# A two-layer decoder on one Trainium2 core: in the second causal attention the softmax division moves from the output to the exponentials, on GpSimd, and the norms' weights are applied while queries and keys are copied

## The chip, the cores and the metric

The kernel runs on one core of one Trainium2 chip. A core has five engines with queues of their own, each worked off in order: TensorE for matrix products (PE in the profile, its weight loads PEld), VectorE (DVE), ScalarE (ACT), GpSimd (POOL) and SyncE (SP), which here starts transfers. PE writes its results to PSUM, which DVE and ACT read; the other tiles lie in SBUF. The metric is device microseconds of one execution, the median of several.

## The reference

Two layers, each of self attention, a second sub-layer against a context, and a feed-forward part; after each of the six, the sum with its input is normalised over the 512 features. The change concerns the second layer's causal self attention alone (32 heads of 16 features, 8 sequences of 128 tokens; `x` is `(8, 128, 512)`):

```python
def _layer_norm(x, w, b):
    mu = jnp.mean(x, axis=-1, keepdims=True)
    var = jnp.mean(jnp.square(x - mu), axis=-1, keepdims=True)
    return (x - mu) * jax.lax.rsqrt(var + LN_EPS) * w + b
qkv = jnp.clip(jnp.einsum('bsd,ed->bse', hidden_states, Wqkv), -CLIP_QKV, CLIP_QKV)
q, k, v = jnp.split(qkv, [D_MODEL, 2 * D_MODEL], axis=-1)
q = _layer_norm(q, q_ln_w, q_ln_b)
k = _layer_norm(k, k_ln_w, k_ln_b)
...
scores = jnp.einsum('bqhd,bkhd->bhqk', q, k) * HEAD_DIM ** (-0.5)
scores = scores + slopes[None, :, None, None] * rel[None, None]
scores = jnp.where(causal[None, None], scores, jnp.float32(-1e+30))
probs = jax.nn.softmax(scores, axis=-1)
out = jnp.einsum('bhqk,bkhd->bqhd', probs, v).reshape(B, S, D_MODEL)
return jnp.einsum('bsd,ed->bse', out, Wout)
```

## The kernel before

All arithmetic is in fp32. The program is written as a sequence of instructions for named engines. The framework's planner then fixes each engine's order: of the instructions that its own cost estimates hold to be ready, the one written first goes first; `issue_after` puts an instruction behind another on its engine. It also puts in the waits between engines.

**The loop of the second attention** (the last loop that the printed functions show, over `b` and `f in (0, 2)`) makes two passes for each of the 8 batch items. A pass treats 16 heads, as two blocks of 128 features ("units"), with the class `Heads16`, which the first layer's attention uses too:

- Its constructor makes the scores: 32 small matrix products (L164) of a block of `qT` (queries turned, features by tokens) and of `kbd`. `kbd` holds the turned keys twice, each time with one of every two heads set to zero, so that one product serves two heads. DVE adds the bias (L672) into the tile `e` and takes the maxima (L181), each in two halves of the four row groups `r`. A row of `e` has 384 columns: two heads by 128 keys for the later 64 queries ("part" 0), two heads by 64 keys for the earlier ones (part 1).
- `exps(half)`: eight exponentials on ACT (L193), in place, each with its sum into `su`.
- `turn()`, one pass later: the reciprocal of the sums (DVE, L202), copied out to 16 columns a head by POOL (`rb`, L205); 12 transposes of `e` on PE (L212), copied to `pT` by DVE and ACT (L213); two transposes of `rb` on PE (L218), copied to `rT` by ACT (L220).
- `out()`, two passes later: probabilities times values (L229, L235), and the product with `rT` on DVE (L240) into `oT`. So the division of the softmax is done on the output, transposed.

Between these, each pass prepares the next item. In pass f=0: `normed` for queries and for keys. PE makes the projection (L86), DVE clips it (L627), takes the moments (L91 to L95), POOL the power (`rs`, L97), DVE subtracts the mean and scales (L631), and POOL multiplies by the norm's weights (L632) and adds its offsets (L633). `lnv` holds the four vectors of 512, the same in all partitions; it is loaded once (L609), and its two parts for queries are scaled by POOL (L611). The keys' last steps are put among the next pass's maxima (`keys_late`). In pass f=2: `values` (L646), the turned tokens of the item after, and `turned_both`: four transposes of the queries, copied to `qT` by DVE (L137); four of the keys, which DVE copies to `kbd` in one product with `pair`, the two masks of heads (L657). `projection` multiplies the previous item's `oT` by the output weights in two halves (L665), around `turned_both`, then adds and normalises (L103, L91 to L107).

`ps1` has four PSUM banks used in turn by most products; `ps2` two pairs of banks, used in turn by the scores and by the transposes of `e`.

Of the kernel before, what the change touches and what calls it, by code (L numbers as in the profile page):

```python
# [11 lines left out]
F32 = mybir.dt.float32  # L12
AF = mybir.ActivationFunctionType
ALU = mybir.AluOpType
# [3 lines left out]
P = 128  # L18
B, S, D = 8, 128, 512
NC = D // P  # L20
H, HD = 32, 16
# [17 lines left out]
def bc(ap, shape):  # L39
    return ap.to_broadcast(shape)  # L40
# [3 lines left out]
def decoder(ctx: ExitStack, tc: tile.TileContext, a: dict, out: bass.AP):  # L44
    nc = tc.nc
# [4 lines left out]
    sm = ctx.enter_context(tc.tile_pool(name="sm", bufs=4))  # L50
# [6 lines left out]
    def bank(name):  # L57
        return ps1.tile([P, 512], F32, tag="ps1", name=name)
# [14 lines left out]
    ident = glob.tile([P, P], F32, tag="ident", name="ident")  # L73
# [6 lines left out]
    pair = masks[:, C_HEAD : C_HEAD + 2]  # L80
# [65 lines left out]
    class Heads16:  # L146
# [5 lines left out]

        W = 3 * P

        def __init__(self, pool, units, bias, o_dst, name, between=()):
            self.pool, self.units, self.o_dst, self.name = pool, units, o_dst, name
            s = [banks(f"s_{name}_{i}") for i in range(2)]
            for part, cols, keys in ((0, slice(0, 2 * P), P), (1, slice(2 * P, 3 * P), 64)):  # L160
                for r in range(4):
                    rows = slice(32 * r, 32 * r + 32)
                    for u, (qT, kbd, _, _) in enumerate(units):
                        nc.tensor.matmul(  # L164
                            s[r // 2][64 * u : 64 * u + 64, r % 2, cols],
                            lhsT=qT[rows, 64 - 64 * part : P - 64 * part], rhs=kbd[rows, :, :keys],
                            start=True, stop=True,
                        )
# [19 lines left out]
        def exps(self, half):  # L188
            for part in range(2):
                e = self.by_heads(part)  # L190
                for r in (2 * half, 2 * half + 1):
                    for x in range(2):
# [2 lines left out]
                            bias=self.m[:, part, r, x : x + 1], accum_out=self.su[:, part, r, x : x + 1],  # L195
                        )

        def turn(self):


            rc = sm.tile([P, 16], F32, tag="rc", name=f"rc_{self.name}")
            nc.vector.reciprocal(rc, self.su.rearrange("p a r x -> p (a r x)"))  # L202

            rb = self.pool.tile([P, 2, 8, HD], F32, tag="rb", name=f"rb_{self.name}", bufs=1)
            nc.gpsimd.tensor_copy(rb, bc(rc.rearrange("p (a h) -> p a h", a=2).unsqueeze(3), [P, 2, 8, HD]))  # L205
            self.pT = self.pool.tile([P, 4, self.W], F32, tag="pT", name=f"pT_{self.name}", bufs=1)
            for i in range(2):
                pt = banks(f"pt_{self.name}_{i}")
                for r in range(2):
                    for k in range(3):  # L210
                        cols = slice(k * P, (k + 1) * P)
                        nc.tensor.transpose(pt[:, r, cols], self.e[:, 2 * i + r, cols], ident)  # L212
                (nc.scalar.copy if i else nc.vector.tensor_copy)(  # L213
                    self.pT[:, 2 * i : 2 * i + 2, :], pt[:, :, : self.W]
                )
            pr = bank(f"pr_{self.name}")
            for a in range(2):
                nc.tensor.transpose(pr[:, a * P : (a + 1) * P], rb[:, a].rearrange("p h d -> p (h d)"), ident)  # L218
            self.rT = self.pool.tile([P, 2, P], F32, tag="rT", name=f"rT_{self.name}", bufs=1)
            nc.scalar.copy(self.rT, pr[:, : 2 * P].rearrange("p (a q) -> p a q", a=2))  # L220

        def out(self):
            o = bank(f"o_{self.name}")
            for u, (_, _, v, vd) in enumerate(self.units):
                v, vd = (t() if callable(t) else t for t in (v, vd))
                late = slice(u * P + 64, u * P + P)
                for x in range(2):
                    for r in range(4):
                        nc.tensor.matmul(  # L229
                            o[32 * r : 32 * r + 32, late],  # L230
                            lhsT=v[:, 48 * r + 16 * x : 48 * r + 16 * x + 32],
                            rhs=self.pT[:, r, x * P + 64 * u : x * P + 64 * u + 64], start=(x == 0), stop=(x == 1),
                        )
                for r in range(4):
                    nc.tensor.matmul(  # L235
                        o[32 * r : 32 * r + 32, u * P : u * P + 64],
                        lhsT=vd[:, 32 * r : 32 * r + 32],
                        rhs=self.pT[:, r, 2 * P + 64 * u : 2 * P + 64 * u + 64], start=True, stop=True,
                    )
            nc.vector.tensor_tensor(  # L240
                self.o_dst.rearrange("p u (a q) -> p u a q", a=2),
                o[:, : 2 * P].rearrange("p (u a q) -> p u a q", u=2, a=2),
                self.rT[:, ::-1].rearrange("p a (u q) -> p u a q", u=2),
                ALU.mult,
            )
# [251 lines left out]
    for n, (p, f) in enumerate(steps):  # L497
        if f == 0:
            oTs.append(ap.tile([P, 2, NC, P], F32, tag="oT", name=f"oT0_{p}"))
        qT, kbd = qk  # L500
        units = []
# [4 lines left out]
        now = Heads16(ap, units, causal_bias, oTs[p][:, :, f, :], f"a0_{p}_{f}")  # L506
# [40 lines left out]
    kp = layer.enter_context(stage("a1k", 1))  # L547
# [57 lines left out]

    alibi = kp.tile([P, 2, 4, 3 * P], F32, tag="alibi", name="alibi")
    nc.sync.dma_start(alibi, a["alibi"])
    lnv = kp.tile([P, 4, D], F32, tag="lnv", name="lnv")
    nc.sync.dma_start(lnv, a["L1_ln"].partition_broadcast(P))  # L609

    nc.gpsimd.tensor_scalar(lnv[:, 0:2, :], lnv[:, 0:2, :], SCALE, None, ALU.mult)  # L611

    v_bufs = [values_tiles(qp, i) for i in range(2)]

# [5 lines left out]
    def normed(i, b, xT, later=None):  # L620


        n, w = (("q", w1q), ("k", w1k))[i]
        pq = bank(f"p{n}1_{b}")
        mm_acc(pq, [(xT[:, c, :], w[:, c, :]) for c in range(NC)])
        q = qp.tile([P, D], F32, tag=n, name=f"{n}1_{b}")
        nc.vector.tensor_scalar(q, pq, 8.0, -8.0, ALU.min, ALU.max)  # L627
        mean, rs = moments(q, f"{n}1_{b}")

        def normalized():  # L630
            done = nc.vector.tensor_scalar(q, q, mean, rs, ALU.subtract, ALU.mult)  # L631
# [17 lines left out]

    def turned_both(b, q, k):  # L650
        qT = ap.tile([P, NC, P], F32, tag="qT", name=f"qT1_{b}")
        transposed(q, NC, P, qT, f"qT1_{b}", "v")
        pt = bank(f"pTk1_{b}")
        for c in range(NC):
            nc.tensor.transpose(pt[:, c * P : (c + 1) * P], k[:, c * P : (c + 1) * P], ident)
        kbd = ap.tile([P, 2, D], F32, tag="kbd", name=f"kbd1_{b}")
        nc.vector.tensor_tensor(kbd, bc(pt.unsqueeze(1), [P, 2, D]), bc(pair.unsqueeze(2), [P, 2, D]), ALU.mult)  # L657
        return qT, kbd

    def projection(b, oT):  # L660
# [64 lines left out]
    v = values(0, xT)  # L725
# [75 lines left out]
    for b in range(B):  # L801
        qT, kbd = qk
        v_now = v
        oT = ap.tile([P, NC, P], F32, tag="oT", name=f"oT1_{b}")
        for f in (0, 2):
            units = []
# [19 lines left out]
                front.go(1)  # L826
            if prev:
                prev.turn()
            now.exps(1)
            half = projection(b - 1, oT_before) if f == 2 and b else iter((0, 0))  # L830
            next(half)
            if b + 1 < B:
                if f == 0:
                    raw.append(normed(1, b + 1, xT, keys_late))
                else:
                    qk = turned_both(b + 1, *raw)
            if b == B - 1:
                front.go(1)
            next(half)
# [314 lines left out]
def _layouts(i):  # L1154
# [16 lines left out]
        "vecs": np.stack(  # L1171
            [cols(i[k]) for k in ("L0_attn_bq", "L0_attn_bk")], axis=1
        ),
        "L1_ln": np.stack([i[f"L1_attn_{k}"] for k in ("q_ln_w", "q_ln_b", "k_ln_w", "k_ln_b")]),
        "L0_bvo": np.stack([i["L0_attn_bv"], i["L0_attn_bo"]]),
        "F0_base": _rows(i["L0_ffn_base_W"]),
        "F0_lora": np.concatenate(
# [7 lines left out]
            axis=1,  # L1185
# [38 lines left out]
```

## Time and profile before

| | us |
|---|---|
| median of the runs shown (902.07, 903.83, 905.71) | 903.83 |
| the profiled execution | 900.43 |
| its span, first to last instruction | 898.5 |
| PE busy in it | 863.2 (96%) |
| DVE busy | 564.9 (63%) |
| ACT busy | 361.7 (40%) |
| POOL busy | 166.1 (18%) |

The busy shares are means over stages with different limits; for a change in one stage the stage's own rows count. The second attention takes about 323 to 510 us. A row of the timeline gives start, duration, engine, line, operation, names of the tiles written and read, partitions by elements, and in brackets how long the engine had been idle before and whom it waited for. DVE instructions overlap a little: the next one can start some 0.1 us before the end of the row above. The groups by line give busy time and, after the comma, the mean duration in ns.

### The profile page before, as it was taken

The page shows a single profiled execution, that of the slowest core. Times are in us where ns is not written, and L with a number is a line of the kernel's source. Part 1 is how long each engine was busy: PE and PEld are TensorE (multiplying, and loading weights), DVE is VectorE, ACT ScalarE, POOL GpSimd, SP SyncE. Part 2 cuts the span into 40 slices and gives each one's busy share as a digit, 9 for nine tenths or more (in the row PEclk, how much of TensorE's full clock was granted, in tenths as well). Part 3 has the DMA queues.
Part 4 walks back from the last instruction along what each step waited for, and adds up shares of the span by engine and source line. Part 5 has one row for each costly group of instructions (what it writes and reads, how often), then busy time and mean ns, then how long its engine had stood idle before and what let it go on. Part 6 is the DMA issues. An engine that isn't in the chain of part 4 may idle for free.

```text
span 898.5 us, 16975 instructions
## 1 busy us (share of the span) xinstructions
PE 863.2 (96%) x6494; PEld 535.1 (60%) x6494; DVE 564.9 (63%) x1310; ACT 361.7 (40%) x1517; POOL 166.1 (18%) x235
## 2 busy tenths in 40 slices
PE   9999999999899999999999999999999999989985
PEld 5766655654455455555556687756576566764542
DVE  3757787776969567888888405635454444456744
ACT  3787464654222115766666313213122212233210
POOL 2401233132533413333333000000000000000001
PEclk9999999999999999999999999999999999989898
DMA  9700000130300002000012210422232212124220
GB/s 330 314 2 25 2 18 9 47 106 1 153 1 24 1 1 95 2 1 1 2 43 101 63 34 15 103 47 48 47 72 48 54 42 57 43 46 102 72 71 35
DMA packets 29779, 51.19 MB, mean 57 GB/s; under 512 B 5250, under 2 KB 21762, under 8 KB 27778
## 3 DMA queue, kind: packets, MB, share of 16 engines
q1 hardware_dynamic: 27138, 48.00, 17.9%
q10 hardware_dynamic: 2560, 2.10, 1.1%
q8 instruction: 51, 0.84, 0.4%
q14 instruction: 30, 0.25, 0.1%
HBM read 31.21 MB, written 2.10 MB: 37 GB/s over the span
## 4 chain that ended last, share of the span: by engine, by line
PE 68%; DVE 16%; ACT 9%; SPq 3%; issue 1%; POOL 1%; DMA 1%; POOLq 0%; DVEq 0%; ACTq 0%
PE pox L86 9%; ACT e_a L193 5%; PE pq L86 5%; PE pkx L86 5%; PE pqx L86 5%; PE pk L86 4%; PE pv L86 4%; PE o_x L924 4%; PE pof L86 4%; PE pvx L86 3%; SPq L914 3%; PE pt_a L212 3%; PE s_x L879 3%; PE po L665 2%; PE s_a L164 2%; DVE e_x L907 2%
## 5 line engine op out<-in xcount | busy, mean ns | idle before, releaser
L193 ACT ACTIVATE e_a<-e_a,m_a 128x128 f32<-128x128 f32 (+1 forms) x512 | 184.8, 365 | 113.7 <-DVE m_a L181 113.7
L900 ACT ACTIVATE e_x<-s_x,m_x 128x256 f32<-128x256 f32 x128 | 58.6, 483 | 141.6 <-DVE m_x L890 107.5
L193 ACT ACTIVATION_READ_ACCUMULATOR e_a<-e_a,m_a 128x1 f32 x512 | 97.6, 191 | 0.0
L86 PE MATMUL pox<-w_X_o,oTx 128*128 128x512 f32 x192 | 84.5, 597 | 0.0
L86 PE MATMUL pqx<-xTx,w_X_q 128*128 128x256 f32 x384 | 84.3, 380 | 0.0
L86 PEld LDWEIGHTS pqx<-xTx,w_X_q 128*128 128x128 f32 x384 | 72.7, 190 | 10.8 <-issue 1.0
L889 DVE TENSOR_REDUCE m_x<-s_x 128x4 f32<-128x1024 f32 x32 | 37.6, 1215 | 49.6 <-PE s_x L879 49.6
L86 PEld LDWEIGHTS pox<-w_X_o,oTx 128*128 128x128 f32 x192 | 35.8, 190 | 48.8 <-issue 48.8
L181 DVE TENSOR_REDUCE m_a<-e_a 128x4 f32<-128x512 f32 (+1 forms) x128 | 62.6, 542 | 0.0
L97 POOL TENSOR_TENSOR rs_x<-ve_x,neghalf 128x1 f32<-128x1 f32 x8 | 4.4, 548 | 307.6 <-DVE ve_x L95 307.6
L879 PE MATMUL s_x<-kTx,qTx 32*128 32x256 f32 x768 | 52.3, 391 | 3.3 <-ACT e_x L900 3.3
L212 PE MATMUL pt_a<-ident,e_a 128*128 128x128 f32 x384 | 48.6, 274 | 4.9 <-DVE e_a L352 3.9
L879 PEld LDWEIGHTS s_x<-kTx,qTx 32*128 32x128 f32 x768 | 41.4, 188 | 16.6 <-issue 9.2
L212 PEld LDWEIGHTS pt_a<-ident,e_a 128*128 128x128 f32 x384 | 43.5, 141 | 12.8 <-DVE e_a L352 4.9
L103 DVE TENSOR_TENSOR x_x<-pox,x_a 128x512 f32<-128x512 f32 x8 | 5.5, 691 | 65.7 <-PE pox L86 65.7
L924 PE MATMUL o_x<-pT_x,vx 128*32 128x512 f32 x384 | 43.3, 595 | 1.4 <-DVE oTx L930 1.4
L908 DVE STREAM_TRANSPOSE e_x<-e_x 128x1024 f32<-128x1024 f32 x32 | 39.7, 1240 | 0.8
L792 ACT COPY qTx<-pqx 128x512 f32<-128x512 f32 x24 | 14.1, 589 | 63.2 <-PE pqx L86 63.2
L907 DVE TENSOR_SCALAR e_x<-e_x,rc_x 128x256 f32<-128x256 f32 x128 | 36.3, 347 | 3.4 <-DVE rc_x L904 1.8
L164 PEld LDWEIGHTS s_a<-kbd,qT 32*64 32x64 f32 x1024 | 20.8, 131 | 28.0 <-issue 8.9
L164 PE MATMUL s_a<-kbd,qT 32*64 32x256 f32 (+1 forms) x1024 | 33.3, 335 | 1.7 <-DVE pT_a L213 0.8
L202 DVE RECIPROCAL rc_a<-su_a 128x16 f32<-128x16 f32 x32 | 8.0, 251 | 40.5 <-ACT e_a L193 40.5
(206 smaller groups left out, 1647.3 us busy)
## 6 DMA issues: line engine op xcount, KB each, us to landing
pT_x<-e_x SPq DMA_DIRECT2D x224, 64.0 KB, 2.0
w_X_q<-in_X_q SPq DMA_DIRECT2D x3, 1024.0 KB, 5.2
w_X_o<-in_X_o SPq DMA_DIRECT2D x3, 1024.0 KB, 5.0
w_L_Wv<-in_L_Wv SPq DMA_DIRECT2D x2, 1024.0 KB, 6.2
w_L_Wo<-in_L_Wo SPq DMA_DIRECT2D x2, 1024.0 KB, 7.8
x_in<-in_x SPq DMA_DIRECT2D x8, 256.0 KB, 8.5
ct<-in_ctx SPq DMA_DIRECT2D x8, 256.0 KB, 4.4
cT<-in_ctxT SPq DMA_DIRECT2D x4, 512.0 KB, 3.9
```

Source lines behind the costliest of these rows:

```text
L86: nc.tensor.matmul(ps, lhsT=l, rhs=r, start=(i == 0), stop=(i == n - 1))
L164: nc.tensor.matmul(s[r // 2][64 * u : 64 * u + 64, r % 2, cols], lhsT=qT[rows, 64 - 64 * part : P - 64 * part], rhs=kbd[rows, :, :keys], s ...
L181: self.scored = nc.vector.tensor_reduce(self.m[:, part, rs, :], self.by_heads(part)[:, rs], AX.X, ALU.max, negate=True)
L193: nc.scalar.activation(e[:, r, x, :], e[:, r, x, :], AF.Exp, bias=self.m[:, part, r, x : x + 1], accum_out=self.su[:, part, r, x : x + 1],)
L212: nc.tensor.transpose(pt[:, r, cols], self.e[:, 2 * i + r, cols], ident)
L879: nc.tensor.matmul(sc[g // 2][:, g % 2, u * 256 : (u + 1) * 256], lhsT=qT[rows, (h0 + u) * NS + n, :], rhs=kT[rows, n], start=(n == 0), st ...
L889: nc.vector.tensor_reduce(m, self.s[i], AX.X, ALU.max, negate=True)
L900: nc.scalar.activation(self.e[:, :, j, :], self.s[half][:, i, :].rearrange("p (a k) -> p a k", k=32), AF.Exp, bias=self.m[:, j : j + 1], s ...
L907: nc.vector.tensor_scalar(e, e, self.rc[:, j : j + 1], None, ALU.mult)
L908: nc.vector.transpose(self.e[:, :, js, :], self.e[:, :, js, :])
L914: queues[j % len(queues)].dma_start(pT[32 * j : 32 * j + 32, :, i, self.h0 // 2, :], e[32 * i : 32 * i + 32, :, j, :])
L924: nc.tensor.matmul(po[32 * g : 32 * g + 32, :], lhsT=v[:, s, g * XD + 32 * n : g * XD + 32 * n + 32], rhs=pT[:, s].rearrange("p i h x -> p ...
```

## The change

Four things are changed.

- `Heads16` gets a method `divide(half)`: the reciprocal of the half's eight sums on DVE, then two products on POOL, in place in `e`, one for each part, with the reciprocal broadcast along the keys. Where it has been called (`rc` is set), `turn()` makes no `rb`, no transposes of it and no `rT`, and `out()` copies instead of multiplying. The first layer's attention doesn't call it and stays as it is.
- The loop of the second attention calls `divide(0)` before the second half's exponentials are written, and `divide(1)` behind `normed` for the keys (f=0) or `turned_both` (f=2).
- `normed` no longer multiplies and adds the norms' vectors on POOL.
- `turned_both` applies them, now one value a partition, as it copies from PSUM: four instructions on DVE for `qT`, eight for `kbd` (a block of 128 features by a mask of heads), whose factors and offsets, `lnk`, are `lnv` times the masks. `lnv` is loaded as 4 x 4 values a partition instead of 4 x 512.

```diff
+        def divide(self, half):
+            rs = slice(2 * half, 2 * half + 2)
+            if self.rc is None:
+                self.rc = sm.tile([P, 2, 4, 2], F32, tag="rcd", name=f"rc_{self.name}")
+            nc.vector.reciprocal(self.rc[:, :, rs, :], self.su[:, :, rs, :])
+            for part in range(2):
+                e = self.by_heads(part)[:, rs]
+                nc.gpsimd.tensor_tensor(e, e, bc(self.rc[:, part, rs, :].unsqueeze(3), list(e.shape)), ALU.mult)
+
         def turn(self):
-            rc = sm.tile([P, 16], F32, tag="rc", name=f"rc_{self.name}")
-            nc.vector.reciprocal(rc, self.su.rearrange("p a r x -> p (a r x)"))
-
-            rb = self.pool.tile([P, 2, 8, HD], F32, tag="rb", name=f"rb_{self.name}", bufs=1)
-            nc.gpsimd.tensor_copy(rb, bc(rc.rearrange("p (a h) -> p a h", a=2).unsqueeze(3), [P, 2, 8, HD]))
+            if self.rc is None:
+                rc = sm.tile([P, 16], F32, tag="rc", name=f"rc_{self.name}")
+                nc.vector.reciprocal(rc, self.su.rearrange("p a r x -> p (a r x)"))
+
+                rb = self.pool.tile([P, 2, 8, HD], F32, tag="rb", name=f"rb_{self.name}", bufs=1)
+                nc.gpsimd.tensor_copy(rb, bc(rc.rearrange("p (a h) -> p a h", a=2).unsqueeze(3), [P, 2, 8, HD]))
...
+            if self.rc is not None:
+                return
             pr = bank(f"pr_{self.name}")
...
+            if self.rc is not None:
+                nc.vector.tensor_copy(self.o_dst, o[:, : 2 * P].rearrange("p (u q) -> p u q", u=2))
+                return
             nc.vector.tensor_tensor(
...
-    lnv = kp.tile([P, 4, D], F32, tag="lnv", name="lnv")
-    nc.sync.dma_start(lnv, a["L1_ln"].partition_broadcast(P))
-
+    lnv = kp.tile([P, 4, NC], F32, tag="lnv", name="lnv")
+    nc.sync.dma_start(lnv, a["L1_ln"])
     nc.gpsimd.tensor_scalar(lnv[:, 0:2, :], lnv[:, 0:2, :], SCALE, None, ALU.mult)
+    lnk = kp.tile([P, 2, 2, NC], F32, tag="lnk", name="lnk")
+    for x in range(2):
+        nc.gpsimd.tensor_scalar(lnk[:, x], lnv[:, 2:4, :], pair[:, x : x + 1], None, ALU.mult)
...
         def normalized():
-            done = nc.vector.tensor_scalar(q, q, mean, rs, ALU.subtract, ALU.mult)
-            nc.gpsimd.tensor_tensor(q, q, lnv[:, 2 * i, :], ALU.mult)
-            nc.gpsimd.tensor_tensor(q, q, lnv[:, 2 * i + 1, :], ALU.add)
-            return done
+            return nc.vector.tensor_scalar(q, q, mean, rs, ALU.subtract, ALU.mult)
...
     def turned_both(b, q, k):
         qT = ap.tile([P, NC, P], F32, tag="qT", name=f"qT1_{b}")
-        transposed(q, NC, P, qT, f"qT1_{b}", "v")
+        pt = bank(f"pTq1_{b}")
+        for c in range(NC):
+            nc.tensor.transpose(pt[:, c * P : (c + 1) * P], q[:, c * P : (c + 1) * P], ident)
+        for c in range(NC):
+            nc.vector.tensor_scalar(
+                qT[:, c, :], pt[:, c * P : (c + 1) * P], lnv[:, 0, c : c + 1], lnv[:, 1, c : c + 1], ALU.mult, ALU.add
+            )
         pt = bank(f"pTk1_{b}")
         for c in range(NC):
             nc.tensor.transpose(pt[:, c * P : (c + 1) * P], k[:, c * P : (c + 1) * P], ident)
         kbd = ap.tile([P, 2, D], F32, tag="kbd", name=f"kbd1_{b}")
-        nc.vector.tensor_tensor(kbd, bc(pt.unsqueeze(1), [P, 2, D]), bc(pair.unsqueeze(2), [P, 2, D]), ALU.mult)
+        for c in range(NC):
+            for x in range(2):
+                cols = slice(c * P, (c + 1) * P)
+                nc.vector.tensor_scalar(
+                    kbd[:, x, cols], pt[:, cols], lnk[:, x, 0, c : c + 1], lnk[:, x, 1, c : c + 1], ALU.mult, ALU.add
+                )
         return qT, kbd
...
             if prev:
                 prev.turn()
+            now.divide(0)
             now.exps(1)
...
                 else:
                     qk = turned_both(b + 1, *raw)
+            now.divide(1)
             if b == B - 1:
                 front.go(1)
```

(The arrays made ahead of the launch hold the four norm vectors by features accordingly.)

More of the change, by code (lines that the diff above doesn't have):

```diff
@@ L157, in __init__ @@
         def __init__(self, pool, units, bias, o_dst, name, between=()):
-            self.pool, self.units, self.o_dst, self.name = pool, units, o_dst, name
+            self.pool, self.units, self.o_dst, self.name, self.rc = pool, units, o_dst, name, None
             s = [banks(f"s_{name}_{i}") for i in range(2)]
@@ L1173, in _layouts @@
         ),
-        "L1_ln": np.stack([i[f"L1_attn_{k}"] for k in ("q_ln_w", "q_ln_b", "k_ln_w", "k_ln_b")]),
+        "L1_ln": np.stack([cols(i[f"L1_attn_{k}"]) for k in ("q_ln_w", "q_ln_b", "k_ln_w", "k_ln_b")], axis=1),
         "L0_bvo": np.stack([i["L0_attn_bv"], i["L0_attn_bo"]]),
```

## The prediction

> **What bounds the kernel now.** I read the page first: PE is busy for 96% of the span, the chain that ended last is 68% PE, 16% DVE and 9% ACT. The change touches only the second causal attention, roughly 323 to 510 us, so I read that stretch alone. The table by windows (us, then PE, PEld, DVE, ACT and POOL busy with counts, clock, DMA share, GB/s):
>
> ```profile
> 370.00:395.00 25.00, 25.00 (x252) 14.96 (x251) 20.57 (x41) 17.38 (x88) 11.01 (x15) 1.00 0.01 2
> 395.00:420.00 25.00, 25.00 (x292) 14.48 (x294) 20.71 (x40) 16.84 (x82) 8.27 (x12) 1.00 0.01 2
> ```
>
> PE has no gap at all, at full clock; DVE is next with 83%; GpSimd has room. One batch item takes two passes (f=0 and f=2). Scores start at 397.08 and again at 418.87: a period of 21.79 us. The chain of waits through the second pass:
>
> ```profile
> 414.41 0.22 PE pr_a L218 x2
> 414.63 1.72 PE po L665 x4
> 416.35 0.44 PE pt_qT L129 x4
> 416.78 0.44 PE pTk L655 x4
> 417.22 1.72 PE po L665 x4
> 418.94 0.84 PE s_a L164 x32
> ```
>
> Between the keys' transposes and the next scores there are 1.72 us of other PE work; in that time DVE must have made qT and kbd. The timeline of DVE shows how close this is:
>
> ```profile
> 404.02 0.55 DVE L107 TENSOR_SCALAR x_a<-x_a,mv_a,rs_a 128x512 f32<-128x512 f32 x1
> 404.48 0.69 DVE L91 BATCH_NORM_STATS2 st_q<-q 128x6 f32<-128x512 f32 x1
> 406.96 0.55 DVE L631 TENSOR_SCALAR q<-q,mv_q,rs_q 128x512 f32<-128x512 f32 x1 [0.66 <-POOL rs_q L97]
> 407.83 0.25 DVE L202 RECIPROCAL rc_a<-su_a 128x16 f32<-128x16 f32 x1 [0.33 <-ACT e_a L193]
> 414.04 0.67 DVE L646 TENSOR_SCALAR v<-pv 128x512 f32<-128x512 f32 x1
> 414.64 0.94 DVE L213 COPY pT_a<-pt_a 128x768 f32<-128x768 f32 x1
> 416.82 0.69 DVE L137 COPY qT<-pt_qT 128x512 f32<-128x512 f32 x1 [1.24 <-PE pt_qT L129]
> 417.43 1.21 DVE L657 TENSOR_TENSOR kbd<-pTk,masks 128x1024 f32<-128x1024 f32 x1
> 419.49 0.25 DVE L202 RECIPROCAL rc_a<-su_a 128x16 f32<-128x16 f32 x1 [0.85 <-ACT e_a L193]
> 420.21 1.81 DVE L672 TENSOR_TENSOR e_a<-s_a,alibi 128x768 f32<-128x768 f32 x2
> ```
>
> kbd ends at 418.64, 0.23 before the scores at 418.87. From the biased scores at 398.51 to those at 420.21 DVE has 21.70 us, of which it is idle 0.66 + 0.33 + 1.24 + 0.85 = 3.08 (the brackets); 18.62 are occupied.
>
> **Off PE.** The two transposes of rb (L218) go: 0.22 a pass, 16 passes, 3.5 us; 0.44 of each period. That would leave 21.35 us a period, and is all that PE gains.
>
> **Off and onto POOL.** Four multiplications and additions an item at 1.27 and two copies of rb at 0.40 go: 5.9. Each divide is one product of 128x512 and one of 128x256, with a broadcast factor. L431 is the same form and takes 1.04; the half size lies between 0.40 (the copy of 128x256) and 0.64 (half of 1.27), I take 0.55. Four divides an item: 6.4, against 5.9, so POOL stays near 40%. What counts is lateness. The exponentials of f=0 end at 407.7 and are transposed from 412.94; those of f=2 end at 419.5 and are transposed from 424.05. Reciprocal 0.25, products 1.59 and some 0.2 of semaphores make 2.05 us, which fits under 5.2 and 4.5. The cover is PE's projections; a divide later than that by x would cost PE x in each pass. At the stage's end the reciprocal starts at 501.83 and the transposes at 504.19: 2.36 against 2.05, which just fits (0 to 0.5 us, I take 0). Behind the first divide on POOL stands rs_q: in the row above DVE waits 0.66 for it. The first divide can start no earlier than the eighth exponential (404.06) and, if its reciprocal is queued behind st_q, ends near 406.9, so rs_q may come 0 to 0.45 late.
>
> **Onto DVE.** The copy of qT (gap to the next start 0.61) and kbd (1.21 less 0.08 of overlap) go: 1.74. Twelve instructions of 128x128 from PSUM with two per-partition scalars come. The trace has none such. Nearest rows:
>
> ```profile
> L968 DVE SCALAR_TENSOR_TENSOR ls<-pl,rc,lg 128x128 f32<-128x128 f32 x8 | 2.8, 348 | 0.2
> L587 DVE TENSOR_SCALAR gx<-gx,rcg 128x28 f32<-128x28 f32 x8 | 1.8, 231 | 0.1
> 647.79 1.14 DVE L907 TENSOR_SCALAR e_x<-e_x,rc_x 128x256 f32<-128x256 f32 x4 [0.22 <-DVE rc_x L904]
> L431 POOL TENSOR_TENSOR ex<-ex,rcw 128x512 f32<-128x512 f32 x8 | 8.3, 1041 | 21.9 <-DVE rcw L430 18.5 <-DVE gx L582 3.4
> ```
>
> L968 is the size and source with one scalar of that kind: 0.35. What a second costs: L587 (28 columns, 0.231) and L907 (256 columns, 0.347 each) have one and give 0.51 ns a column and 0.217 fixed; L107 has two and 512 columns, 0.546 - 512 x 0.51 ns = 0.285 fixed, so 0.07 more. One of the twelve lasts 0.42 and the next starts some 0.09 earlier (L968, L907 and L107 all overlap their follower so): 0.33. Bounds: 0.21 without scalars (L646 starts its follower after 0.60 for 512 columns, L672 after 0.86 for 768; 1.02 ns a column), and 0.42 without overlap. I take 0.33: 3.96 an item. The reciprocals become four of eight values instead of two of sixteen, +0.17 each way round, 0.34 an item (before, 0.17 from start to start). The copy of 128x256 that replaces the product at L240 costs the same as it, within 0.05. ACT loses the copy of rT (0.36 a pass), but ACT idles over 3 us a pass, so this is nothing.
>
> Occupied time on DVE: 18.62 - 1.74 + 3.96 + 0.34 = 21.18; with the wait for rs_q of 0.66, which nothing fills, 21.84, or 22.29 with rs_q 0.45 late. **The queue that PE waits in** is longer too: scores of the next f=0 need four instructions of qT and the first four of kbd (blocks 0 and 1). From the scores to the start of qT it was 416.82 - 397.08 = 19.74, now 19.30; then 7 x 0.33 + 0.42 + 0.07 = 2.80: a period of 22.10. So PE's gain is used up in both loops: 22.10 to 22.29, I take 22.20, +0.41 for each of the seven items whose successor is normalised.
>
> The Trainium skill, "VectorE: DVE Perf Modes", section "The DRAIN you can't avoid", speaks against cutting one instruction into many: it says that the next instruction does not start until the pipeline is empty. The rows agree that each has a fixed cost, but not with the rule's strict form, as 404.48 lies before the end of 404.02 + 0.55. By the strict rule the block would cost 5.0 instead of 3.96 an item.
>
> **Elsewhere.** The load of lnv shrinks, and its scaling (L611, 2.78 us on POOL) nearly goes; beside it a DVE instruction of L580 took 1.10 instead of 0.23 at 236.48, and PE waited 1.11 behind that: 0 to -0.87, I take -0.4. In item 0 PE idled 0.97 for POOL's addition to k (L633), but the next matmuls waited for ACT's copy of pT as well: 0 to -0.97, I take -0.4. Item 7 has no successor and keeps PE's 0.44.
>
> **Sum.** 7 x 0.41 - 0.44 - 0.4 - 0.4 = +1.6 us. The profiled execution took 900.43 (span 898.5), so 902.0; the median of the runs shown is 903.83, 3.4 above, so 905.4. About 0.5% (4.5 us) is what a measurement of this kernel can tell from no change.
>
> **Rivals.** (A) PE keeps its gain. The planner put other matmuls ahead of late scores once before:
>
> ```profile
> 353.21 0.47 PE L229 MATMUL o_a<-pT_a,v 128*32 128x64 f32 x14
> 224.35 1.89 DVE L107 TENSOR_SCALAR x_a<-x_a,mv_a,rs_a 128x512 f32<-128x512 f32 x1 [0.67 <-POOL rs_a L97]
> ```
>
> (the scores followed only at 355.17). With that 0.78 in front and 0.21 an instruction the period is 21.35: 8 x -0.44 - 0.8 = -4.3, 899.5. Against it: the fixed cost of the scalars shows in four rows. (B) The other side: DVE becomes the bound. At 0.42 each, 18.62 - 1.74 + 5.04 + 0.34 + 0.66 = 22.92, with rs_q late 23.37; 23.1 gives 7 x 1.3 - 1.2 = +8, 912. It decides (beyond 0.5%) once an instruction takes over 0.36. The same time follows if the scores wait for all twelve: 19.30 + 11 x 0.33 + 0.49 = 23.42, 914. Against the latter: the exponentials at 401.00 start before the maxima of the other half are done at 402.07, so waits go by parts of a tile. (C) The divides hold DVE's normalisations. The second row of the last fence is L107 beside POOL's fills: 1.89 instead of 0.55. Three such instructions run an item; one hit an item gives 7 x 1.34 + 1.6, 914. Against it: by the timeline each of them falls before a divide starts or after it ends. The Trainium skill, "GPSIMD Engine Reference", section "Key points", names contention of GpSimd with two-port VectorE instructions; the row fits it, and with the rule on every normalisation it would be three hits.
>
> **How the numbers follow.** Forecast 0.52 (901 to 909), A 0.15, B 0.20, C 0.13. The range reaches to A's 899.5 and past B's 912: 899.5 to 913. Faster by over 0.5% takes half of A and a little, 0.09; slower takes B, C and the forecast's upper edge, 0.39; within, 0.52.
>
> **What would show it.** Right: no L218 in this stage; qT and kbd rows of 128x128 near 0.42 with starts 0.33 apart; PE idle before s_a of 0.3 to 0.8 an item, released by kbd; a period of 22.1 to 22.3. A: a period under 21.6 and out ahead of the scores. B: DVE above 95% from 370 to 470. C: L107 or L631 over 1 us beside POOL products. Wrong in another way: transposes of e that wait for POOL.

## The result, and the profile after

| | before | after |
|---|---|---|
| median of 20 runs each, us | 904.16 (901.01 to 906.33) | 908.19 (904.84 to 910.19) |
| ratio, 95% interval | 1 | 1.0042 (1.0029 to 1.0056) |
| span of the profiled execution, us | 898.5 | 903.3 |
| an item of the loop, scores to scores, us | 21.79 | 22.53 |
| PE busy in 370 to 420 us | 50.00 | 48.89 |
| DVE busy in 370 to 420 us | 41.28 | 45.44 |

The kernel became 0.4% slower: about 4 us, inside the range and slightly inside what counted as no change, but more than twice the forecast +1.6 us. (The ratio is estimated from the single runs; the quotient of the two medians is 1.0045.) The table by windows of the changed kernel (columns as before):

```profile
370.00:395.00 25.00, 24.60 (x241) 14.14 (x240) 22.48 (x53) 16.01 (x81) 10.01 (x16) 1.00 0.01 2
395.00:420.00 25.00, 24.29 (x246) 13.53 (x244) 22.96 (x57) 16.01 (x79) 10.06 (x15) 1.00 0.00 1
```

PE has gaps where it had none, and DVE went from 83% to 91%. The chain of waits through one period (start, length, engine, tile, line), followed back from the maxima of one item, tells more:

```profile
404.83 0.87 DVE pT_a L224
405.70 0.45 DVE x_a L107
406.15 0.60 DVE st_q L91
406.75 0.10 DVE rc_a L203
406.86 0.12 DVE mv_q L93
...
407.00 1.04 POOL e_a L206
408.04 0.52 POOL rs_q L97
...
408.58 0.83 DVE q L651
...
413.63 2.99 ACT e_a L194 x16
...
416.64 0.20 DVE rc_a L203
416.84 0.82 DVE pT_a L224
417.66 1.27 DVE qT L673 x4
418.94 2.55 DVE kbd L683 x8
421.49 0.11 DVE rc_a L203
```

Before, the chain through the same stretch was PE in every piece. Now it holds no PE at all: it runs along DVE's queue, leaves it for GpSimd (a product of the first divide, then the queries' 1/std behind it), comes back, leaves it for ScalarE's exponentials, comes back. Once round is 22.53 us. The whole page shows the same shift: PE's share of the chain that ended last fell from 68% to 60%, DVE's rose from 16% to 24%.

The timeline of the changed kernel, with the rows that the prediction named:

```profile
418.96 0.41 PE L242 MATMUL o_a<-pT_a,v 128*32 128x64 f32 x10
419.72 1.44 PE L165 MATMUL s_a<-kbd,qT 32*64 32x256 f32 x32 [0.35 <-DVE kbd L683]
...
495.88 0.91 PE L165 MATMUL s_a<-kbd,qT 32*64 32x256 f32 x32 [1.46 <-ACT pT_a L224]
...
407.00 0.15 DVE L95 TENSOR_SCALAR ve_q<-mv_q 128x1 f32<-128x1 f32 x1
408.58 0.83 DVE L651 TENSOR_SCALAR q<-q,mv_q,rs_q 128x512 f32<-128x512 f32 x1 [1.42 <-POOL rs_q L97]
...
416.64 0.20 DVE L203 RECIPROCAL rc_a<-su_a 128x8 f32<-128x8 f32 x1 [0.47 <-ACT e_a L194]
...
417.58 1.36 DVE L673 TENSOR_SCALAR qT<-pTq,lnv 128x128 f32<-128x128 f32 x4
418.86 2.63 DVE L683 TENSOR_SCALAR kbd<-pTk,lnk 128x128 f32<-128x128 f32 x8
...
407.00 1.04 POOL L206 TENSOR_TENSOR e_a<-e_a,rc_a 128x512 f32<-128x512 f32 x1 [1.54 <-DVE mv_q L93]
408.00 0.55 POOL L97 TENSOR_TENSOR rs_q<-ve_q,neghalf 128x1 f32<-128x1 f32 x1
408.51 0.61 POOL L206 TENSOR_TENSOR e_a<-e_a,rc_a 128x256 f32<-128x256 f32 x1
```

The rows of before that belong to it (DVE twice, then POOL):

```profile
405.08 0.94 DVE L213 COPY pT_a<-pt_a 128x768 f32<-128x768 f32 x1
406.15 0.15 DVE L95 TENSOR_SCALAR ve_q<-mv_q 128x1 f32<-128x1 f32 x1
406.38 0.55 POOL L97 TENSOR_TENSOR rs_q<-ve_q,neghalf 128x1 f32<-128x1 f32 x1 [2.40 <-DVE ve_q L95]
```

Three things are seen. The queries' variance is ready at 407.15 (407.00 + 0.15), but GpSimd began the divide's first product at 407.00, so 1/std starts at 408.00, and DVE waits 1.42 instead of 0.66; before, 1/std started 0.08 after the variance (406.30, 406.38). DVE's normalisation then lasts 0.83 instead of 0.55, beside GpSimd's second product. And the first scores of an item wait for `kbd`, with ten matmuls of `out` already put ahead of them.

Where the 4.8 us between the two spans came from, by the starts of the scores: the first scores of the stage come 0.95 earlier (330.52 against 331.47); items 0 and 1 take 0.31 more; items 2 to 6 take 112.67 instead of 108.51, 4.16 more; from item 7's first scores to the first scores of the next sub-layer it is 60.68 instead of 60.16, 0.52 more; what follows there, which the change doesn't touch, was 0.74 longer. Two of these terms are not the loop's. Of the 0.95, 0.52 were there before `lnv` is loaded (transposes of `e` at 211.48 came at 210.96). And over all the profiles of this document the last stretch lay between 354.6 and 357.8 us, so below the period is read from the profiles and the time from the medians.

### The profile page after: what moved, and what is told of

Its sections match the earlier page's. It is cut to its first block, busy times and chain, and to the rows that moved or that the text cites. A ratio compares the mean times of both kernels' runs of the same rounds, so it can differ in the third digit from the quotient of the medians.

```text
span 903.3 us, 17027 instructions
## 1 busy us (share of the span) xinstructions
PE 863.6 (96%) x6462; PEld 533.2 (59%) x6462; DVE 582.1 (64%) x1406; ACT 357.7 (40%) x1501; POOL 169.7 (19%) x253
## 4 chain that ended last, share of the span: by engine, by line
PE 60%; DVE 24%; ACT 10%; POOL 2%; issue 1%; SPq 1%; DMA 0%; POOLq 0%; DVEq 0%; ACTq 0%
PE pox L86 9%; PE pqx L86 8%; ACT e_a L194 7%; PE pkx L86 5%; PE s_x L909 4%; PE o_x L954 4%; PE pof L86 4%; PE pvx L86 3%; PE pq L86 3%; DVE e_a L700 3%; DVE m_a L182 2%; PE pk L86 2%; PE pv L86 2%; DVE kbd L683 2%; PE pt_a L223 1%
## 5 line engine op out<-in xcount | busy, mean ns | idle before, releaser
L206 POOL TENSOR_TENSOR e_a<-e_a,rc_a 128x512 f32<-128x512 f32 x64 | 51.8, 826 | 50.1 <-DVE rc_a L203 36.7
L165 PE MATMUL s_a<-kbd,qT 32*64 32x256 f32 (+1 forms) x1024 | 36.0, 335 | 5.6 <-DVE kbd L683 2.6
```

The costliest lines, as they stand in the source:

```text
L165: nc.tensor.matmul(s[r // 2][64 * u : 64 * u + 64, r % 2, cols], lhsT=qT[rows, 64 - 64 * part : P - 64 * part], rhs=kbd[rows, :, :keys], s ...
L206: nc.gpsimd.tensor_tensor(e, e, bc(self.rc[:, part, rs, :].unsqueeze(3), list(e.shape)), ALU.mult)
```

## The experiments

Two groups of waits could explain 22.53 instead of the 21.35 us that PE's own work would take: those of the weights (twelve copies, scores waiting for `kbd`) and those of the division (1/std behind the product, reciprocals ahead of other work). Three theories stand against each other in the first three runs: T (DVE's queue is the bound), D (the divides are the price), K (only the copies' latency ahead of the scores counts); the fourth has T and D.

| run | period, us | median, us | ratio to before, 95% |
|---|---|---|---|
| division only | 22.19 | 906.87 | 1.0045 (1.0024 to 1.0065) |
| weights only | 24.13 | 918.16 | 1.0164 (1.0145 to 1.0183) |
| after, divide queued later | 21.88 | 903.35 | 1.0001 (0.9990 to 1.0012) |
| after, constants for the vectors | 22.19 | 905.12 | 1.0026 (1.0015 to 1.0036) |
| after, later divide, copies sorted | 21.36 | 900.93 | 0.9973 (0.9955 to 0.9991) |
| weights only, sums early | 22.31 | 908.27 | 1.0056 (1.0035 to 1.0077) |
| division only, later divide | 21.84 | 906.68 | 1.0038 (1.0020 to 1.0056) |
| after, later divide in f=0 only | 21.87 | 904.28 | 1.0017 (1.0003 to 1.0030) |
| after, copies sorted only | 22.53 | 907.72 | 1.0057 (1.0037 to 1.0078) |
| after, later divide, copies split | 22.62 | 910.39 | 1.0089 (1.0070 to 1.0109) |

The runs of before beside them had medians of 902.57 (first four rows), 902.22 (next four) and 902.42 (last two). The ratios are again estimated from the single runs and are not quotients of the medians; in the fifth row that quotient would be 0.9986.

**1. The division only.** Weights on GpSimd and the two copies as before the change; `divide` as in the change.

```diff
-            return nc.vector.tensor_scalar(q, q, mean, rs, ALU.subtract, ALU.mult)
+            done = nc.vector.tensor_scalar(q, q, mean, rs, ALU.subtract, ALU.mult)
+            nc.gpsimd.tensor_tensor(q, q, lnv[:, 2 * i, :], ALU.mult)
+            nc.gpsimd.tensor_tensor(q, q, lnv[:, 2 * i + 1, :], ALU.add)
+            return done
```

> Only the division on GpSimd; the norms' weights stay on POOL, qT and kbd are copied as before. Theory T (DVE's queue sets the period: the changed kernel's 22.54 us an item are 20.65 of DVE work and 1.89 of waits, of which the twelve copies cost 3.84 where 1.74 stood): without the copies DVE has 18.62 + 0.24 + waits of 1.4 + 0.5 + 0.3, about 21.0, under PE's 21.35, so the period is near 21.4 and the time 2 to 4 us under the kernel before, unless POOL (14 us of work an item, the weights' products among them) makes PE wait for the keys' transposes. Rival D (the divides are the price, the copies are hidden): the period stays near 22.5 and the time 3 to 4 us over before. Rival K (the copies' latency alone, from the transposes to the scores): period 21.35, time 3.5 us under before.

It measured 22.19 us an item, ratio 1.0045. Its timeline, PE and then DVE:

```profile
418.33 0.66 PE L673 MATMUL pTk<-ident,k 128*128 128x128 f32 x4 [0.61 <-POOL k L651]
...
409.52 0.83 DVE L649 TENSOR_SCALAR q<-q,mv_q,rs_q 128x512 f32<-128x512 f32 x1 [1.62 <-POOL rs_q L97]
```

Without any of the twelve copies the late 1/std (1.62) and the held normalisation (0.83) are there, and a new wait: PE's transposes of the keys wait 0.61 for GpSimd, where the products of the divide stand between the keys' weights. So the division costs time by itself: T's 21.4 and K's 21.35 us were missed, D's 22.5 us and 3 to 4 us over before come nearest.

**2. The weights only.** `divide` is not called; the division stays on the output.

```diff
-            now.divide(0)
...
-            now.divide(1)
```

> Only the norms' weights at the copies; the softmax division stays on the output. Theory T: DVE has 18.62 - 1.74 + 3.84 = 20.72 and the wait of 0.66 for rs_q, 21.4, under PE's 21.79; the scores wait for qT and kbd, 19.74 + 0.07 + 2.1 to 2.7, so the period is 21.9 to 22.3 and the time 0 to 3 us over before. Rival D: no change from before, 0 within 1 us. Rival K: period 22.5 or more (PE still has its 0.44 of transposes in front), time 5 us over before.

It measured 24.13 us an item. T and D missed it, and K, whose "22.5 or more" takes it in, had 5 us over before where 15 came. The timeline shows why:

```profile
409.43 0.44 PE L231 MATMUL pr_a<-ident,rb_a 128*128 128x128 f32 x2 [1.60 <-POOL rb_a L216]
...
408.25 0.24 DVE L213 RECIPROCAL rc_a<-su_a 128x16 f32<-128x16 f32 x1
```

The planner now put the reciprocal of the sums at 408.25, behind the bias, the maxima and the moments, where before it stood directly behind `kbd` (419.49 in the prediction's rows). GpSimd spreads it only then, and PE's transposes of `rb` wait 1.60. That wait belongs neither to the changed kernel, which has no such transposes, nor to the kernel before. As a price of the twelve copies this run says nothing; run 6 repeats it without the wait.

**3. The divide queued later.** The changed kernel, with the first half's reciprocal put behind the queries' normalisation on DVE (f=0) and behind DVE's copy of `pT` (f=2). Nothing else.

```diff
+            behind = normed.done if f == 0 and b + 1 < B else prev.copied if prev else None
+            with tc.issue_after(behind.ins) if behind else nullcontext():
-            now.divide(0)
+                now.divide(0)
```

> The changed kernel, with the first half's reciprocal queued on DVE behind the queries' normalisation (f=0) and behind the copy of pT (f=2), so that POOL's power for the queries (rs_q) no longer stands behind the first half's product. Theory T: the wait for rs_q falls from 1.42 to 0.66, the normalisation from 0.83 to 0.55, the wait of 0.47 ahead of pT's copy goes; the period falls from 22.54 by 0.8 to 1.5 to 21.1 to 21.7, the time by 5 to 9 us against the changed kernel: 2 to 5 us under the kernel before. Rival K: the period stays at 22.3 to 22.5. Rival D (POOL's divides late for the transposes): it rises, since the first half's products come later.

It measured 21.88 us an item, ratio 1.0001: the whole loss is gone. T's 21.1 to 21.7 us and its 2 to 5 us under the kernel before were not reached; K (no change) and D (a longer item) fall. From its timeline, DVE and PE:

```profile
406.67 0.55 DVE L653 TENSOR_SCALAR q<-q,mv_q,rs_q 128x512 f32<-128x512 f32 x1 [0.66 <-POOL rs_q L97]
...
417.81 0.41 PE L244 MATMUL o_a<-pT_a,v 128*32 128x64 f32 x10
418.16 1.21 PE L165 MATMUL s_a<-kbd,qT 32*64 32x256 f32 x32
```

The wait for 1/std is back at 0.66 and the normalisation at 0.55. What is left over 21.35 is 0.53 around the scores: the 32 matmuls of an item's first scores take 1.21 where the second pass takes 0.91, and `out`, of which ten matmuls stand ahead of them and the rest follows in small groups, takes 1.05 by the chain of waits instead of 0.81.

**4. Constants for the vectors.** The changed kernel, whose twelve copies multiply by 1 and add 0, so that the norms' weights and the masks of heads are left out.

```diff
-                qT[:, c, :], pt[:, c * P : (c + 1) * P], lnv[:, 0, c : c + 1], lnv[:, 1, c : c + 1], ALU.mult, ALU.add
+                qT[:, c, :], pt[:, c * P : (c + 1) * P], 1.0, 0.0, ALU.mult, ALU.add
```

> The changed kernel with constants 1 and 0 in place of the per-partition scalars of the twelve copies: the norms' weights and the masks of heads are left out. If the fixed cost is the scalars' (0.06 to 0.07 each by the rows of before), a copy starts 0.19 to 0.21 after the one before it instead of 0.32, DVE has 1.3 to 1.5 us an item less, and by theory T the period falls to 21.3 or a little above and the time 6 to 8 us against the changed kernel. Rival D: period unchanged at 22.5. If the cost is that of the read from PSUM, the starts stay 0.32 apart and nothing moves.

Period 22.19, ratio 1.0026. The timeline of DVE:

```profile
408.97 0.82 DVE L651 TENSOR_SCALAR q<-q,mv_q,rs_q 128x512 f32<-128x512 f32 x1 [1.63 <-POOL rs_q L97]
...
418.75 1.66 DVE L683 TENSOR_SCALAR kbd<-pTk 128x128 f32<-128x128 f32 x8
```

and, from the timeline of DVE and of PE, then from the chain of waits:

```profile
398.87 0.20 DVE L203 RECIPROCAL rc_a<-su_a 128x8 f32<-128x8 f32 x1 [0.65 <-ACT e_a L194]
...
419.38 1.21 PE L165 MATMUL s_a<-kbd,qT 32*64 32x256 f32 x32 [0.40 <-DVE kbd L683]
```

```profile
407.38 1.04 POOL e_a L206
...
414.01 3.36 ACT e_a L194 x18
...
418.62 0.68 ACT pT_a L224
419.30 1.73 ACT e_a L194 x10
```

Eight copies take 1.66 instead of 2.63, which is 0.20 instead of 0.32 from start to start; the twelve save 1.45 us an item, but the item becomes only 0.34 shorter. Neither T (21.3) nor D (22.5) fits. Part of what is saved turns up again as waits: DVE waits 1.63 instead of 1.42 for 1/std, and 0.65 for ScalarE's exponentials ahead of the reciprocal behind which the next residual sum and bias stand, where the changed kernel has no wait. The chain of waits now holds none of the copies: it runs through the divide's product, the normalisation, the bias, ScalarE's exponentials and that reciprocal. Run 1, which has no such copies, has the same chain and the same 22.19 us. So this is the division's own loop, and it was hidden behind 22.53.

**5. Order, and copies sorted.** Run 3, with the six copies that the first scores need (blocks 0 and 1 of queries and of keys) ahead of the other six; the keys' transposes are therefore written ahead of all the copies.

```diff
-        for c in range(NC):
-            nc.vector.tensor_scalar(
-                qT[:, c, :], pt[:, c * P : (c + 1) * P], lnv[:, 0, c : c + 1], lnv[:, 1, c : c + 1], ALU.mult, ALU.add
-            )
...
+        for pair0 in (0, 2):
+            for c in (pair0, pair0 + 1):
+                nc.vector.tensor_scalar(
+                    qT[:, c, :], pt[:, c * P : (c + 1) * P], lnv[:, 0, c : c + 1], lnv[:, 1, c : c + 1], ALU.mult, ALU.add
+                )
+            for c in (pair0, pair0 + 1):
+                for x in range(2):
...
```

> Keeps the new place of the first half's reciprocal (the run before measured 21.88 us an item with it) and sorts the twelve copies: queries' blocks 0 and 1, keys' blocks 0 and 1 (six instructions, two and four), then blocks 2 and 3. The scores of f=0 read blocks 0 and 1 only, so the second of them is ready two copies, 2 x 0.32 us, earlier. Theory F (the 0.53 us that are left over the 21.35 of TensorE's own work are the first scores' wait for these copies): period 21.3 to 21.5 us, 15 items x 0.45 = 6 to 7 us off the changed kernel on top of the order's gain... that is 0.993 to 0.997 of the kernel before. Rival S (the stretch has another cause, the transposes' place or the planner's order of TensorE): period stays 21.8 to 21.9 and the ratio 0.999 to 1.001.

It measured 21.36 us an item and 900.93 us, ratio 0.9973, with an interval that ends below 1. The period is theory F's; the ratio lies just above F's 0.993 to 0.997, which was worked out with 15 items where the loop has seven such periods. The windows and, below, rows of the timeline of this kernel:

```profile
370.00:395.00 25.00, 25.00 (x252) 14.98 (x251) 23.24 (x55) 16.38 (x84) 9.59 (x15) 1.00 0.01 2
395.00:420.00 25.00, 25.00 (x316) 14.42 (x314) 24.04 (x60) 16.98 (x83) 10.41 (x15) 1.00 0.01 2
```

```profile
418.30 0.91 PE L165 MATMUL s_a<-kbd,qT 32*64 32x256 f32 x32
...
490.93 0.91 PE L165 MATMUL s_a<-kbd,qT 32*64 32x256 f32 x32 [1.98 <-ACT pT_a L224]
```

PE has no gap, the scores take 0.91 with nothing of `out` in front, and PE's 0.44 an item is at last a gain. DVE is busy 47.28 of 50 us, so there is little room left. Only the last item loses (1.98 ahead of its second scores, 0.23 before the change).

**6. Weights only, sums early.** Run 2, with the reciprocal and its spreading issued where the change has `divide(1)` (and two buffers for `rb` instead of one).

```diff
+            now.sums()
```

> The weights at the copies alone, division as before, but the sums' reciprocal and its spreading on GpSimd are issued one half item earlier, where the changed kernel has its second division, so that the transposes of the reciprocal can't wait for them. Theory T (the twelve copies cost what the scores wait for them, the division nothing that its order does not): 21.79 + about 0.5 = 22.2 to 22.4 us an item, ratio 1.003 to 1.008. Rival W (the copies alone cost what the weights-only run showed, 24.13 us, and the wait at the reciprocal's transposes was only its sign): over 23.5 us, ratio above 1.012. Rival N (copies free once nothing else stands in VectorE's way): 21.8, ratio 0.998 to 1.001.

22.31 us an item, ratio 1.0056. This timeline of PE is the weights' price without any divide:

```profile
399.85 0.41 PE L246 MATMUL o_a<-pT_a,v 128*32 128x64 f32 x10
400.19 1.20 PE L165 MATMUL s_a<-kbd,qT 32*64 32x256 f32 x32
```

It is 21.79 + 0.52, the same 0.5 around the same scores as in run 3, and theory T's number. Rival W falls, and with it run 2 as a price of the copies.

**7. Division only, with the later divide.** Run 1 with run 3's edit.

> The division alone (weights by GpSimd and the copies as before the change), with the first half's reciprocal queued behind the queries' normalisation (f=0) and behind VectorE's copy of the turned exponentials (f=2). In the division-only run an item took 22.19 us, with queries' 1/std 1.62 us late and keys' weights on GpSimd 0.61 us late for their transposes. Theory T (GpSimd's order is the division's whole price): the first wait goes back to about 0.7 us; the second stays or shrinks: 21.4 to 21.9 us an item, ratio 0.994 to 1.000. Rival G (GpSimd's load itself binds: 3.3 us of products and 4 x 1 us of weights an item): 22.1 or more, ratio 1.003 or more.

21.84 us an item, as theory T had it, but the ratio of 1.0038 lies above what T expected and where rival G (GpSimd's load binds) had it; G's period of 22.1 or more didn't come. The loop is 0.35 shorter than in run 1. The timeline shows what remained:

```profile
398.28 0.66 PE L675 MATMUL pTk<-ident,k 128*128 128x128 f32 x4 [0.34 <-POOL k L653]
...
416.81 0.55 DVE L651 TENSOR_SCALAR k<-k,mv_k,rs_k 128x512 f32<-128x512 f32 x1 [1.62 <-POOL rs_k L97]
```

Now the keys' 1/std stands behind products on GpSimd, and in item 0 PE waits 2.69 for the keys, 1.72 more than before the change. So with the weights still on GpSimd the division doesn't come free by this edit; the two parts of the change help each other there.

**8. The later divide in f=0 only.**

```diff
-            behind = normed.done if f == 0 and b + 1 < B else prev.copied if prev else None
+            behind = normed.done if f == 0 and b + 1 < B else None
```

> The changed kernel with one of the two edits of the order only: f=0's first reciprocal behind the queries' normalisation; f=2's stays ahead of VectorE's copy of the turned exponentials. Theory Q (the 0.66 us that the order gave back are the late 1/std of the queries): 21.85 to 21.95 us an item, ratio 1.000. Rival R (the reciprocal that waits 0.47 us for ScalarE ahead of the copy has its share): 22.1 to 22.4, ratio 1.002 to 1.004.

21.87 us an item, theory Q's number (the ratio of 1.0017 is a little above the expected 1.000). From the timeline of DVE:

```profile
407.04 0.55 DVE L653 TENSOR_SCALAR q<-q,mv_q,rs_q 128x512 f32<-128x512 f32 x1 [0.67 <-POOL rs_q L97]
...
415.13 0.20 DVE L203 RECIPROCAL rc_a<-su_a 128x8 f32<-128x8 f32 x1 [0.48 <-ACT e_a L194]
```

The reciprocal of f=2 still waits its 0.48 ahead of the copy of `pT`, and costs nothing. The whole 0.66 between 22.53 and 21.87 is the queries' 1/std and the normalisation behind it.

**9. Copies sorted, divide where the change put it.** Run 5 without run 3's edit.

> The changed kernel with its twelve copies sorted (blocks 0 and 1 of queries and keys first), the first half's reciprocal left where the change put it. If the two waits add (theory T: 0.53 us for the copies ahead of the scores and 0.66 us for the late 1/std), an item goes from 22.54 to about 22.0 us and the ratio to before is 1.000 to 1.002. Rival M (the two waits lie one behind the other, so that the longer one alone counts once the other is mended): 21.35 + 0.66 is not reached from above, the period stays at 22.2 us or more, ratio 1.002 to 1.005.

Period 22.53, to the hundredth that of the changed kernel, ratio 1.0057, a little above what rival M expected, and far from the 22.0 of theory T. Timeline, PE and DVE:

```profile
419.09 1.45 PE L165 MATMUL s_a<-kbd,qT 32*64 32x256 f32 x32 [0.50 <-DVE kbd L684]
...
408.59 0.83 DVE L651 TENSOR_SCALAR q<-q,mv_q,rs_q 128x512 f32<-128x512 f32 x1 [1.43 <-POOL rs_q L97]
```

The same edit that took 0.52 off in run 5 takes nothing off here. So 0.53 and 0.66 are no two waits that add up: they are two loops, and the longer one counts. The one off PE takes 22.53 whatever order the copies have (and 22.19 where they are short or absent, runs 4 and 1); with it mended, the one through PE's scores takes 21.88; with that mended too, PE's own work takes 21.36.

**10. Copies split.** Run 5, with the six copies of blocks 2 and 3 behind the next item's second biased scores, meant for the wait of 1.98 at the end.

```diff
+        blocks_late.extend([lambda c=c: query(c) for c in (2, 3)])
+        blocks_late.extend([lambda c=c, x=x: key(c, x) for c in (2, 3) for x in range(2)])
...
-            now = Heads16(ap, units, alibi_bias(f), oT[:, f : f + 2, :], f"a1_{b}_{f}", keys_late)
+            now = Heads16(ap, units, alibi_bias(f), oT[:, f : f + 2, :], f"a1_{b}_{f}", keys_late if f else blocks_late)
```

> Mended order and sorted copies (21.36 us an item, ratio 0.9973 measured), and the six copies of blocks 2 and 3 put behind the next item's second biased scores instead of ahead of its first. In the item period nothing is left to gain (TensorE is never idle there): 21.35 to 21.4 us. Theory E (the stage's end, where the last scores wait 1.98 us for ScalarE's copy behind the exponentials, is late because the copies of blocks 2 and 3 stand ahead of the last item's bias on VectorE): that wait goes below 0.6 us, 1 to 2 us off, ratio 0.995 to 0.997. Rival H (the wait is set by ScalarE alone, or the moved copies come late elsewhere): the wait stays near 2 us or shows up again elsewhere, ratio 0.997 to 0.999.

22.62 us an item and ratio 1.0089: rival H, and worse. The wait at the end fell to 0.88, with another 0.88 just behind it; in the loop, by the timeline of POOL and DVE, this came instead:

```profile
410.10 1.61 POOL L206 TENSOR_TENSOR e_a<-e_a,rc_a 128x512 f32<-128x512 f32 x2 [1.60 <-PE s_a L165]
411.67 0.55 POOL L97 TENSOR_TENSOR rs_q<-ve_q,neghalf 128x1 f32<-128x1 f32 x1
...
422.61 0.20 DVE L203 RECIPROCAL rc_a<-su_a 128x8 f32<-128x8 f32 x1 [1.67 <-ACT e_a L194]
```

With 1.9 us of copies ahead of the second maxima, ScalarE's later exponentials are late, a reciprocal waits 1.67 for them ahead of DVE's other work, and products stand ahead of 1/std again. What sets the wait at the stage's end was not settled: in run 5 ScalarE's copy there stands behind the first half's exponentials, which start only when DVE has worked off the copies, the residual sum and the bias.

## Why the prediction was right, and where it was not

The sign, the verdict and the mechanism (PE's gain used up by DVE, a longer loop) were right; the size was 1.6 instead of about 4 us. That 908.19 lies in the range is no test of the sum, since the range goes from 899.5 to 913 and errors of both signs partly cancelled. Of the signs that the prediction named, the L218 that is gone, the copies' durations and starts and PE's idle 0.35 to 0.40 before the scores came; the period, 22.53, lies outside its 22.1 to 22.3. By its steps:

**Off PE.** Right. The 0.44 an item is real: 21.36 us measured in run 5 against 21.35.

**Off and onto POOL.** The products took 1.04 and 0.61, 1.65 a divide against 1.59; the transposes of `e` never waited for them in the loop, as forecast. **The step that failed** is its last one: "the first divide can start no earlier than the eighth exponential (404.06) and, if its reciprocal is queued behind st_q, ends near 406.9, so rs_q may come 0 to 0.45 late." This took the times from the old timeline, where DVE copies `pT` for 0.94 between `st_q` and the variance, time enough for a product. In the new order that copy stands ahead, the reciprocal follows `st_q` directly, and the variance is ready when the product has just begun. So DVE waits 0.76 longer (1.42 against 0.66), and its normalisation 0.28 longer: 1.04 together. (That this is also the first product's length is chance: the 0.28 belong to the second.) Run 8 takes exactly this away, and 0.66 us an item with it; then the next loop counts.

**Onto DVE.** The copies start 0.319 apart (0.33 forecast). The section of the Trainium skill that the prediction quotes on this ("VectorE: DVE Perf Modes", section "The DRAIN you can't avoid") adds that an instruction which is not held starts earlier, and the rows agree: 0.319 from start to start where one copy lasts 0.40. The reciprocals add 0.12, not 0.34: four at 0.11 to 0.12 to the next start against two at 0.17. Occupied time was put at 21.18; by the rows from one item's biased scores to the next (22.54) it was 22.54 - 1.42 - 0.47 - 0.28 = 20.37. Too much work and too little waiting were assumed, which partly cancelled. (These two rows account for 0.35 of the 0.81 too much; the rest was not traced.)

**The queue that PE waits in** was put at 22.10, and the loop at "22.10 to 22.29, I take 22.20". With nothing else in the way it is 21.88 (run 3) or 21.79 + 0.52 (run 6). The two loops were rightly not added. But the upper one was 22.53 and outside the interval: 0.33 more for each of the five full periods, 1.7 us of the missing 2.4 to 3.2. Another 0.4 is item 6: it turns no tokens and had taken 21.35, where the sum counted from 21.79, and as its loop is now off PE it took 22.53 like the others. In the term 21.88, 0.30 are the longer scores and 0.24 `out`, which the planner takes apart (run 3). The scores are longer in runs 4 and 9 too (1.21 and 1.45), where nothing of `out` stands ahead of them, so the copies do that; sorting them removed both parts.

**Elsewhere.** The smaller `lnv` brought 0.42 where 0.4 was taken: of the 0.95 by which the stage starts earlier, 0.52 stood before its load, and PE's wait behind its scaling is 0.68 instead of 1.11. Item 0 didn't gain 0.4: PE no longer waits 0.97 for the keys, but then 0.37 and 0.70 for the copies of `pT`, which the prediction named as the other wait there; items 0 and 1 came out 0.31 longer. The last item, which was to keep 0.44, lost 0.52: PE waits 1.46 at its second scores for ScalarE's copy of `pT` (0.23 before). That copy stands behind exponentials that start late, because DVE still works off the copies: the bias begins 2.35 after the first scores (489.67, 487.32), before the change 1.04 (484.84, 483.80).

**Rivals.** A (PE keeps its gain) is what run 5 shows to be possible, not what the change did. B's decisive price (over 0.36 an instruction) didn't come; DVE's queue became the bound all the same, at 91% busy and not above 95%: by waits in it together with the copies (shorter copies take 0.34 off, the shorter wait 0.66, each until another loop counts). C (the divide holds a normalisation) came in small: 0.28 an item instead of 1.34, beside the 0.61 product alone. (C's sum gives 914.8, not 914.) "By the timeline each of them falls before a divide starts or after it ends" was again read from the old order. The Trainium skill, "GPSIMD Engine Reference", section "Key points", names contention of GpSimd with VectorE instructions in a two-port mode, and the 0.83 against 0.55 here fits it; in which mode the normalisation runs no run shows.

## What to carry to other kernels

When work is put on an engine that also serves a short, urgent instruction of another engine, place it by that instruction: 1.04 us of product ahead of a 0.55 us power cost 0.66 us an item, and with that order mended and the copies sorted the change is worth some 0.3% (0.1 to 0.45%) instead of costing 0.4%. Read from the new order, not from the old timeline, what will stand in front; once a second engine is nearly full, its queue keeps no slack that could hide it. And test edits in pairs: sorting the copies brought nothing alone and 0.52 us an item after the order was mended, as the longest of several loops hides the others.

## What the runs showed of the hardware

- A per-partition factor and offset cost a VectorE copy of 128x128 from PSUM 0.12 us: 0.32 from start to start with them, 0.20 with constants (run 4).
- VectorE's normalisation of 128x512 within SBUF took 0.55 with no product of GpSimd beside it and 0.82 to 0.83 beside GpSimd's 128x256 product, in every full period of the four kernels where the two meet there (after, runs 1, 4 and 9). The one time that it ran beside the 128x512 product (item 1 of run 10) it took 1.25.
- GpSimd's product with a broadcast factor took 1.04 for 128x512 and 0.61 for 128x256, less than its product of two full tiles of 128x512 (1.27).
